# Moving the direct term of a state-space scan from VectorE to GpSimd and TensorE

## Chip, cores and metric

The kernel runs on one core of a Trainium2 chip. The metric is device time in microseconds for one launch; the runs shown are three executions of the same program. All arithmetic is in float32. Engine names in profile lines: PE is TensorE's matmul, PEld its weight load, DVE is VectorE, ACT is ScalarE, POOL is GpSimd, SP is SyncE with the DMA queue.

## What is computed

The reference runs two layers over 16 images of 128 channels and 56 x 56 pixels. The first is a vision block with windowed attention and an MLP. The change touches the second layer alone: a 3x3 convolution whose output, read as rows of 8 tokens of 16 values, goes through a small selective-scan (Mamba) block, then a group norm, a SiLU and a residual. Cut to what matters:

```python
def _mamba(seq, ...):
    xz = jnp.einsum('nld,ed->nle', seq, in_proj_w)
    xi, z = jnp.split(xz, 2, axis=-1)
    xc = ...                                   # causal conv over the tokens, then silu
    dt, Bm, Cm = ...                           # projections of xc; dt through softplus
    dA = jnp.exp(dt[..., None] * A)
    dBx = dt[..., None] * Bm[:, :, None, :] * xc[..., None]
    def step(h, inp):
        a, b, c = inp
        h = a * h + b
        return (h, jnp.sum(h * c[:, None, :], axis=-1))
    _, ys = jax.lax.scan(step, h0, ...)        # 8 tokens, 32 x 16 states
    ym = ys.transpose(1, 0, 2) + D * xc
    ym = ym * jax.nn.silu(z)
    return jnp.einsum('nld,ed->nle', ym, out_proj_w)
```

The state starts at zero, so at the first token the recurrence only injects. At the last token the state is not needed any more beyond the output. The kernel uses this: at tokens 0 and 7 the part of the output that comes from the token's own injection, `sum over s of C[s] * B[s] * dt * x`, is formed directly as `(sum of C*B) * (dt*x)`. This is the direct term, `ud` in the code.

## The kernel before

The second layer (`layer1`) works on 112 groups, 7 per image, each of 448 columns (a column is one sequence of 8 tokens). Each group takes 14 steps; step `k` of group `i` handles token `1 + k // 2` and half `k % 2` of the inner channels (`jp`). The 8 tokens lie in two halves `h` (tokens 0 to 3 and 4 to 7): tiles such as `dt`, `dtx`, `xc`, `zs`, `ym` are 128 x 2 x 448, and a partition holds one token of the half and one inner channel.

In every step, in this order:

- DVE: **advance** (L1001: decay times state, in PSUM; at token 7 L999 writes the product as the state), **complete** (L1006: adds the injected part; not at token 7), **inject** for four steps later (L991: the spread `dt*x` from PSUM times B).
- PE: **decay** for two steps later (L973, two matmuls on 32 rows each), **spread** for five steps later (L984, likewise).
- ACT: the exponential of the decay (L976, in place in PSUM).
- POOL, in odd steps: **weigh** (L1010: state times C, 128 x 1792).

Decay has two PSUM buffers and spread has one, so PE's spread waits for the injection before it, and the next injection waits for that spread.

Around these, `work(i, k)` returns lists for PE (with the ACT work that follows a matmul), DVE and POOL, which prepare the next groups and finish the last ones. The lists are issued in the step in which they are named, and `_chain` fixes program order on each engine, so the order by hand is the order on the engines. DVE's list stands after advance and before complete, except in step 0, where it stands after inject. With `prev`, `nxt` and `far` for the group before, the next one and the one after that, the parts are:

- steps 0, 1: `gather` of tokens 5, 6 and 7 of `prev` (L1019: sums over states into PSUM bank `pq[1]`); steps 1, 2: `rate` of `nxt` (L905); step 3: `gate` (L931), and `collect` of half 1 of `prev` (L1032); step 4: `gated` of half 1 (L1035, POOL), and `inner` for `zs` (L892, SiLU with a table load on ACT before and after, L146);
- steps 5, 6: `project_out` of `prev` (L1053); steps 5 to 9: nine convolution taps for the next image (L184); steps 6 and 8: `rate_sum`, four POOL products each (L922 to L925);
- step 7: `skip` of half 0 (L1025: a diagonal matmul adds `D * xc`, and starts the sum in `pq[1]`); steps 8, 9, 10: `gather` of tokens 1, 2, 3; steps 9, 10: `statistics` of the group norm (L1080) in groups that follow an odd or the last group of an image;
- step 10: `product` of `nxt` (L951, C times B); step 11: `sequences` (L884); step 12: `collect` of half 0 and `inner` for `xc` (table loads again); step 13: `direct` of `nxt` (L955: a matmul sums C times B over the states for tokens 0 and 7 into `pq[0]`), `skip` of half 1, `gather` of token 4, and `gated` of half 0.

`direct_mul` (L960), in step 0 on DVE, forms `ud` for both halves from `pq[0]`: bank times a column mask (`vec[:, 6 + h]`, 1 on the partitions of token 0 or of token 7) times `dtx`. `collect` adds `ud` to the gathered sum as it moves it from PSUM to `ym`; `gated` multiplies by `zs`, the SiLU of z.

In four of the seven groups of an image (groups 2 to 5, from the second image on) steps 4 and 12 also run a piece of the normalise-and-SiLU of the image before on ACT (L1121); POOL adds the residual in pieces (L1126). The last image has no convolution taps to run.

Of the kernel before, what the change touches and what calls it, by code (L numbers as in the profile page):

```python
# [10 lines left out]
F32 = mybir.dt.float32  # L11
U32 = mybir.dt.uint32
AF = mybir.ActivationFunctionType
ALU = mybir.AluOpType
# [3 lines left out]
P = 128  # L18
# [5 lines left out]
BLK = 448  # L24
NBLK = HW // BLK
# [113 lines left out]
def _load(nc, pool, ap, name):  # L139
    t = pool.tile(list(ap.shape), F32, tag=name, name=name)  # L140
    nc.sync.dma_start(t, ap)
    return t
# [653 lines left out]
def layer1(ctx: ExitStack, tc: tile.TileContext, x1, t, out, conv):  # L796
# [15 lines left out]
    nc = tc.nc  # L812
# [3 lines left out]
    cst = ctx.enter_context(tc.tile_pool(name="l1c", bufs=1))  # L816
    w1 = ctx.enter_context(tc.tile_pool(name="l1w1", bufs=1))
    w2 = ctx.enter_context(tc.tile_pool(name="l1w2", bufs=2))
# [14 lines left out]
    vec = conv.vec  # L833
    ident = _load(nc, cst, t["k_ident"], "ident1")
# [6 lines left out]
    for w, name in ((wx, "b_kx"), (wv, "b_dtw")):  # L841
        k = w1.tile(list(w.shape), F32, tag="fold", name=name)
# [3 lines left out]
    nc.vector.scalar_tensor_tensor(adec, adec, -1.0, mask, ALU.mult, ALU.mult)  # L846
    dd = cst.tile([P, P], F32, tag="dd", name="dd")
    nc.vector.tensor_scalar_mul(dd, ident, d_w)
    eps = cst.tile([P, 1], F32, tag="eps1", name="eps1")
    nc.vector.memset(eps, GN_EPS)  # L850
    neg = cst.tile([P, 1], F32, tag="neg", name="neg")
# [3 lines left out]
    pq = [ps_q.tile([P, 512], F32, tag=f"q{k}", name=f"pq{k}") for k in range(2)]  # L855
# [97 lines left out]
    def direct(p):  # L953

        nc.tensor.matmul(pq[0][:, 0:BLK], lhsT=cbm, rhs=p["cb"], start=True, stop=True)  # L955

    def direct_mul(p):
        ud = p["ud"] = w2.tile([P, 2, BLK], F32, tag="ud", name=f"ud_{p['n']}")
        for h in range(2):
            nc.vector.scalar_tensor_tensor(  # L960
                ud[:, h, :], pq[0][:, 0:BLK], vec[:, 6 + h : 7 + h], p["dtx"][:, h, :], ALU.mult, ALU.mult
            )

# [58 lines left out]
    def skip(p, h):  # L1024
        nc.tensor.matmul(  # L1025
            pq[1][:, 0:BLK], lhsT=dd, rhs=p["xc"][:, h, :], start=True, stop=False, skip_group_check=True
        )

    def collect(p, h):
        if h == 0:  # L1030
            p["ym"] = w1.tile([P, 2, BLK], F32, tag="ym", name=f"ym_{p['n']}")
        nc.vector.tensor_add(p["ym"][:, h, :], pq[1][:, 0:BLK], p["ud"][:, h, :])  # L1032

    def gated(p, h):
        nc.gpsimd.tensor_mul(p["ym"][:, h, :], p["ym"][:, h, :], p["zs"][:, h, :])  # L1035

    xrs = {}

# [70 lines left out]
    def residual(b, k):  # L1109
        pool, tag = (w2, "xr") if b == NB - 1 and k == 1 else (w1, "res")  # L1110
        res = norms[b, k] = pool.tile([P, half], F32, tag=tag, name=f"res_{b}_{k}")
        nc.sync.dma_start(res[0:64], x1[b][0:64, k * half : (k + 1) * half])
        if k == 0:
            nc.sync.dma_start(res[64:P], x1[b][64:P, 64 : half + 64])
        else:
            nc.sync.dma_start(res[64:P, 0 : half - 64], x1[b][64:P, half + 64 : HW])
            nc.sync.dma_start(res[64:P, half - 64 : half], x1[b][64:P, 0:64])
# [35 lines left out]
    def work(i, k):  # L1153


        def at(n):
            return groups[n] if 0 <= n < len(groups) else None

        p, nxt, far, prev = at(i), at(i + 1), at(i + 2), at(i - 1)
        pe, dve, pool = [], [], []  # L1160

        if prev:
            if k == 0:
                pe += [partial(gather, prev, 5), partial(gather, prev, 6)]
            if k == 1:
                pe.append(partial(gather, prev, 7))
            if k == 3:
                dve.append(partial(collect, prev, 1))
            if k == 4:
                pool.append(partial(gated, prev, 1))  # L1170
            if k in (5, 6):
                pe.append(partial(project_out, prev, k - 5))
            b = prev["b"]
            if prev["g"] % 2 and k in (9, 10):
                dve.append(partial(statistics, b, prev["g"] - 10 + k))
            if prev["g"] == NBLK - 1:
                if k == 9:
                    dve.append(partial(statistics, b, NBLK - 1))
                if k == 12 and b < NB - 1:
                    residual(b, 0)  # L1180
        two = at(i - 2)
        if two and two["g"] == NBLK - 1:
            b = two["b"]
            if k == 3:
                pool.append(partial(deviation, b))
        three = at(i - 3)
        if three and three["g"] == NBLK - 1:
            if k == 1:
                pe.insert(0, partial(group_var, three["b"], 0))
            if k == 2:  # L1190
                pool.append(partial(affine, three["b"]))
                if three["b"] == NB - 1:
                    pool.append(partial(finish, three["b"]))

        eighth = []
        for n in range(3, 7):
            past = at(i - n)
            if past and past["g"] == NBLK - 1 and past["b"] < NB - 1 and k in (4, 12):
                eighth.append(partial(normalise, past["b"], 2 * (n - 3) + k // 12))
        for n in range(4, 8):  # L1200
            past = at(i - n)
            if past and past["g"] == NBLK - 1 and past["b"] < NB - 1 and k == 2:
                pool.append(partial(store, past["b"], (n - 4) // 2, n % 2))
                if n == 5:
                    pool.append(partial(residual, past["b"], 1))

        if p:
            if i == len(groups) - 1 and k in (4, 6):
                residual(p["b"], k // 2 - 2)
            if k == 0:  # L1210
                dve.append(partial(direct_mul, p))
            if k == 7:
                pe.append(partial(skip, p, 0))
            if k in (8, 9, 10):
                pe.append(partial(gather, p, k - 7))
            if k == 12:
                dve.append(partial(collect, p, 0))
            if k == 13:
                if nxt:
                    pe.append(partial(direct, nxt))  # L1220
                pe += [partial(skip, p, 1), partial(gather, p, 4)]
                pool.append(partial(gated, p, 0))
            if k in (2, 6):
                bring(p, 0, {2: (4, 5), 6: (6,)}[k])
            if k in (1, 5, 9):
                bring(p, 1, {1: (3, 4), 5: (5, 6), 9: (7,)}[k])

        if nxt:
            if k in (1, 2):
                pe.append(partial(rate, nxt, k - 1))  # L1230
            if k in (2, 6):
                pe.append(partial(rate_exp, nxt, k // 4))
            if k in (5, 7):
                pe.append(partial(rate_log, nxt, k // 2 - 2))
            if k in (6, 8):
                pool.append(partial(rate_sum, nxt, k // 2 - 3))
            if k == 3:
                pe += [partial(gate, nxt, 0), partial(gate, nxt, 1)]
            if k == 4:
                eighth.insert(0, partial(inner, nxt, "zs", wz, w2, 0.0))  # L1240
            if k == 7:
                bring(nxt, 0, (0, 1))
            if k == 8:
                bring(nxt, 1, (1, 2))
            if k == 11:
                bring(nxt, 0, (2, 3))
            if k == 10:
                pool.append(partial(product, nxt))
            if k == 13 and not p:
                pe.append(partial(direct, nxt))  # L1250

        if p and k in (5, 6, 7, 8, 9) and p["b"] + 1 < NB:
            taps = {5: (0, 1), 6: (2, 3), 7: (4,), 8: (5, 6), 9: (7, 8)}[k]
            pe.append(partial(convolve, p["b"] + 1, p["g"], taps))
        if p and p["g"] == NBLK - 1 and k == 11 and p["b"] + 2 < NB:
            conv.load(p["b"] + 2)
        if two and two["g"] == NBLK - 1 and k == 2:
            pe.append(partial(group_mean, two["b"], 0))
        if far:
            if k == 11:  # L1260
                pe.append(partial(sequences, far))
            if k == 12:
                eighth.insert(0, partial(inner, far, "xc", wx, w3, c1_b))
        if eighth:
            pe = eighth + [partial(_act_set, tc, EXP_LN)] + pe
        return pe, dve, pool
# [10 lines left out]
    start = len(nc.cur_bb.bb.instructions)  # L1277
# [6 lines left out]
    for i in range(-2, len(groups) + 3):  # L1284
        for k in range(14):
            now = 0 <= i < len(groups)
            pe, dve, pool = work(i, k)
# [62 lines left out]
```

## Time and profile before

| | us |
|---|---|
| median of three runs | 8308.35 (8305.95 to 8310.39) |
| profiled execution, its own time | 8305.77 |
| its span, first to last instruction | 8304.0 |
| first and last `direct_mul` start (L960) | 3202.4, 8232.3 |
| mean of a POOL product 128 x 448 (L1035) | 1.145 |
| mean of a weighing 128 x 1792 (L1010) | 4.000 |
| mean of a residual addition 128 x 784 (L1126) | 1.854 |
| mean of a DVE product 128 x 896 (L1001) | 1.091 |
| mean of a statistics instruction (L1080) | 0.618 |
| mean of an ACT copy from PSUM 128 x 448 (L935) | 0.532 |

In lines of groups, after the shapes stand the count, the busy time in us and the mean of one in ns; after the second bar the idle time of the engine before these instructions and what ended it. In timelines a line gives start and duration in us, engine, line, operation, output from inputs, and in brackets the idle time before it. A float32 matmul shows as two records. Line numbers are those of the kernel before.

### The profile page before, as it was taken

To read this page: it belongs to the slowest core of one execution; us is meant where nothing else is said; L and a number is where in the kernel's file an instruction comes from. 1 tells how busy PE (TensorE), PEld (TensorE's weight loads), DVE (VectorE), ACT (ScalarE), POOL (GpSimd) and SP (SyncE) were. 2 spreads that over 40 slices of the span, in tenths; PEclk is the share of its full clock that TensorE was granted. 3 is DMA by queue.
4 is the path that set the end of the run, shared out by engine and by line. 5 is a ranking of instruction groups with operands and counts; after the bars stand their busy time and mean duration, and the time that the engine had idled before them with its cause. 6 is when DMAs were issued, how large, how long until landed. Compare 5 with 4: busy or idle time off the path is not lost.

```text
span 8304.0 us, 151471 instructions
## 1 busy us (share of the span) xinstructions
PE 7835.1 (94%) x52860; PEld 3329.9 (40%) x52860; DVE 7736.9 (93%) x10346; ACT 5642.6 (68%) x10579; POOL 7054.9 (85%) x5692
## 2 busy tenths in 40 slices
PE   5999999999999998999999999999999999999998
PEld 3444444444444453333333333333333333333332
DVE  7999999999999976999999999999999999999998
ACT  4777777777777755666666666666666666666665
POOL 7888788888888725899989999999999989999997
PEclk8999999999999999999999999999999999999998
DMA  3333333333333323333333334334333343334333
GB/s 65 87 86 87 85 89 87 87 87 87 87 87 87 81 79 82 87 93 102 99 92 99 96 91 105 91 97 106 83 104 100 88 105 103 86 99 108 85 93 88
DMA packets 764584, 757.87 MB, mean 91 GB/s; under 512 B 188720, under 2 KB 663984, under 8 KB 761904
## 3 DMA queue, kind: packets, MB, share of 16 engines
q1 hardware_dynamic: 763824, 748.18, 34.9%
q8 instruction: 423, 6.93, 0.4%
q14 instruction: 337, 2.76, 0.1%
HBM read 439.61 MB, written 102.76 MB: 65 GB/s over the span
## 4 chain that ended last, share of the span: by engine, by line
PE 34%; DVE 24%; POOL 24%; issue 9%; ACT 9%; DMA 1%; SPq 0%; POOLq 0%; ACTq 0%; DVEq 0%
PE a L973 7%; DVE h L991 6%; DVE a L1001 5%; POOL cst L1010 5%; PE x L984 5%; POOL xh L315 5%; PE pq L1019 5%; PE pq L892 4%; POOL e L431 4%; DVE h L1006 4%; DVE lepe L512 3%; POOL tap L313 3%; POOL dtx L925 2%; PE pq L931 2%; DVE sst L415 2%
## 5 line engine op out<-in xcount | busy, mean ns | idle before, releaser
L1010 POOL TENSOR_TENSOR cst<-h,cb 128x1792 f32<-128x1792 f32 x784 | 3130.6, 4000 | 348.9 <-DVE h L1006 291.1
L976 ACT ACTIVATE a<-a 128x896 f32<-128x896 f32 x1568 | 1415.7, 903 | 1080.2 <-PE x L984 588.0
L991 DVE TENSOR_TENSOR h<-x,bb 128x896 f32<-128x896 f32 x1568 | 1697.5, 1083 | 96.6 <-PE x L984 58.2
L512 DVE SCALAR_TENSOR_TENSOR lepe<-vpad,lep,lepe 128x448 f32<-128x448 f32 x2688 | 1718.0, 678 | 0.5
L984 PE MATMUL x<-dtx,amask 32*128 32x448 f32 x6272 | 1626.4, 595 | 49.0 <-DVE h L991 38.5
L973 PE MATMUL a<-dt,adec 32*128 32x448 f32 x6272 | 1620.2, 593 | 53.7 <-DVE h L1006 49.9
L1006 DVE TENSOR_TENSOR h<-a,h 128x896 f32<-128x896 f32 x1344 | 1463.1, 1089 | 38.1
L1001 DVE TENSOR_TENSOR a<-a,h 128x896 f32<-128x896 f32 x1344 | 1465.7, 1091 | 26.7 <-ACT a L976 25.8
L431 POOL TENSOR_SCALAR e<-e,sst,zero 128x256 f32<-128x256 f32 x1568 | 861.1, 559 | 466.6 <-DVE sst L427 417.4
L421 ACT ACTIVATE e<-ps,sst 128x256 f32<-128x256 f32 x1568 | 728.6, 469 | 522.5 <-DVE sst L415 470.5
L973 PEld LDWEIGHTS a<-dt,adec 32*128 32x128 f32 x6272 | 474.5, 185 | 1066.5 <-DVE h L1006 501.4
L315 POOL TENSOR_TENSOR xh<-xh,tap 128x448 f32<-128x448 f32 x749 | 859.6, 1148 | 43.7
L184 PE MATMUL pq<-pad,conv 128*128 128x448 f32 x1890 | 834.8, 559 | 0.0
L1019 PE MATMUL pq<-cst,sel 128*32 128x448 f32 x6272 | 734.5, 553 | 0.8 <-POOL cst L1010 0.8
L415 DVE TENSOR_REDUCE sst<-ps 128x2 f32<-128x512 f32 x784 | 540.3, 689 | 107.9 <-PE ps L409 83.0
L146 ACT ACT_TABLE_LOAD x484 | 621.0, 1283 | 9.3 <-PEq L1341 0.7
L453 PE MATMUL ptt<-ident,e 128*128 128x128 f32 x3136 | 538.6, 283 | 93.5 <-POOL e L431 76.8
L984 PEld LDWEIGHTS x<-dtx,amask 32*128 32x128 f32 x6272 | 476.7, 185 | 365.9 <-DVE h L991 344.3
L409 PE MATMUL ps<-sel,q 32*64 32x256 f32 x6272 | 537.3, 411 | 53.2 <-ACT e L421 46.9
L313 POOL TENSOR_SCALAR tap<-pad,pos,zero 128x448 f32<-128x448 f32 x749 | 546.5, 730 | 35.7
L453 PEld LDWEIGHTS ptt<-ident,e 128*128 128x128 f32 x3136 | 366.6, 141 | 417.5 <-POOL e L431 237.0
L459 ACT COPY att<-ptt 128x512 f32<-128x512 f32 x784 | 458.7, 585 | 72.0 <-PE ptt L453 64.1
(175 smaller groups left out, 12040.7 us busy)
## 6 DMA issues: line engine op xcount, KB each, us to landing
sel<-kv SPq DMA_DIRECT2D x3136, 64.0 KB
bb<-db SPq DMA_DIRECT2D x336, 448.0 KB
cb<-dc SPq DMA_DIRECT2D x336, 448.0 KB
pad<-x SPq DMA_DIRECT2D x32, 784.0 KB
x<-r SPq DMA_DIRECT2D x112, 224.0 KB
pad<-x SPq DMA_DIRECT2D x16, 1568.0 KB
db<-bs SPq DMA_DIRECT2D x112, 224.0 KB
dc<-cs SPq DMA_DIRECT2D x112, 224.0 KB
```

What stands on the lines that cost most here:

```text
L315: nc.gpsimd.tensor_add(im["xh"][i], im["xh"][i], held["tap"])
L431: nc.gpsimd.tensor_scalar(e, e, im["st", w][:, 2, p : p + 1], zero, ALU.mult, ALU.add)
L453: nc.tensor.transpose(ptt[:, P * (2 * p + h) : P * (2 * p + h + 1)], e[:, h * P : (h + 1) * P], ident)
L512: nc.vector.scalar_tensor_tensor(out, src, lep[:, k : k + 1], acc, ALU.mult, ALU.add)
L973: nc.tensor.matmul(a[:, k, :], lhsT=adec[rows, l4, :], rhs=p["dt"][rows, h, :], start=True, stop=True)
L976: nc.scalar.activation(p["a", l, jp], p["a", l, jp], AF.Exp)
L984: nc.tensor.matmul(x[:, k, :], lhsT=mask[rows, l4, :], rhs=p["dtx"][rows, h, :], start=True, stop=True)
L991: nc.vector.tensor_mul(p["h", l][:, own(jp), :], px["x"], weight)
L1001: nc.vector.tensor_mul(a, a, before)
L1006: nc.vector.tensor_add(h, p["a", l, jp], h)
L1010: nc.gpsimd.tensor_mul(c, p["h", l], p["gate", 1, l].unsqueeze(1).to_broadcast([P, 4, BLK]))
L1019: nc.tensor.matmul(py[32 * j : 32 * j + 32], lhsT=sel[:, l4, :], rhs=p["c", l][:, j, :], start=False, stop=(l % 4 == 3), skip_group_check= ...
```

## The change

Three things are changed in the second layer.

1. `direct` copies its bank to an SBUF tile `cbs` on ACT right after the matmul. `direct_mul` becomes one POOL product of 128 x 2 x 448, `dtx` times `cbs`, without the mask, still in step 0.
2. The mask becomes a diagonal matrix per half, `ends[:, h, :]`, made once. `skip` issues a second matmul with it, which adds the masked `ud` to `pq[1]`. `collect` then multiplies the bank with `zs` instead of adding `ud`, and `gated` and its two calls go.
3. `statistics` moves from steps 9 and 10 to step 13 and to step 0 of the group after.

```diff
+    ends = cst.tile([P, 2, P], F32, tag="ends", name="ends")
+    for h in range(2):
+        nc.vector.tensor_scalar_mul(ends[:, h, :], ident, vec[:, 6 + h : 7 + h])
...
         nc.tensor.matmul(pq[0][:, 0:BLK], lhsT=cbm, rhs=p["cb"], start=True, stop=True)
+        p["cbs"] = w1.tile([P, BLK], F32, tag="cbs", name=f"cbs_{p['n']}")
+        nc.scalar.copy(p["cbs"], pq[0][:, 0:BLK])

     def direct_mul(p):
-        ud = p["ud"] = w2.tile([P, 2, BLK], F32, tag="ud", name=f"ud_{p['n']}")
-        for h in range(2):
-            nc.vector.scalar_tensor_tensor(
-                ud[:, h, :], pq[0][:, 0:BLK], vec[:, 6 + h : 7 + h], p["dtx"][:, h, :], ALU.mult, ALU.mult
-            )
+        p["ud"] = w1.tile([P, 2, BLK], F32, tag="ud", name=f"ud_{p['n']}")
+        nc.gpsimd.tensor_mul(p["ud"], p["dtx"], p["cbs"].unsqueeze(1).to_broadcast([P, 2, BLK]))
...
             pq[1][:, 0:BLK], lhsT=dd, rhs=p["xc"][:, h, :], start=True, stop=False, skip_group_check=True
         )
+        nc.tensor.matmul(
+            pq[1][:, 0:BLK], lhsT=ends[:, h, :], rhs=p["ud"][:, h, :], start=False, stop=False, skip_group_check=True
+        )
...
-        nc.vector.tensor_add(p["ym"][:, h, :], pq[1][:, 0:BLK], p["ud"][:, h, :])
-
-    def gated(p, h):
-        nc.gpsimd.tensor_mul(p["ym"][:, h, :], p["ym"][:, h, :], p["zs"][:, h, :])
+        nc.vector.tensor_mul(p["ym"][:, h, :], pq[1][:, 0:BLK], p["zs"][:, h, :])
...
-            if k == 4:
-                pool.append(partial(gated, prev, 1))
...
-            if prev["g"] % 2 and k in (9, 10):
-                dve.append(partial(statistics, b, prev["g"] - 10 + k))
             if prev["g"] == NBLK - 1:
-                if k == 9:
-                    dve.append(partial(statistics, b, NBLK - 1))
...
         two = at(i - 2)
+        if prev and prev["g"] % 2 and k == 13:
+            dve.append(partial(statistics, prev["b"], prev["g"] - 1))
+        if two and (two["g"] % 2 or two["g"] == NBLK - 1) and k == 0:
+            dve.append(partial(statistics, two["b"], two["g"]))
...
             if k == 0:
-                dve.append(partial(direct_mul, p))
+                pool.append(partial(direct_mul, p))
...
-                pool.append(partial(gated, p, 0))
```

## The prediction

> **What bounds the kernel now.** I read the engine totals first, then the groups of instructions on the lines the change touches, then the timelines of single groups in the second layer, and last the granted clock in windows of a few us.
>
> ```profile
> PE 7835.1 (94%) x52860; PEld 3329.9 (40%) x52860; DVE 7736.9 (93%) x10346; ACT 5642.6 (68%) x10579; POOL 7054.9 (85%) x5692
> ...
> L991 DVE TENSOR_TENSOR h<-x,bb 128x896 f32<-128x896 f32 x1568 | 1697.5, 1083 | 96.6 <-PE x L984 58.2 <-POOL cst L1010 18.4 <-DMA bb<-db 3.9
> ```
>
> PE and DVE are both near full. Shares do not say which one a step waits for, so the steps must be read. The first product of a group starts at 3202.4 us and that of the 112th at 8232.3: 45.31 us a group, all of it in the second layer, which alone is changed.
>
> ```profile
> L960 DVE SCALAR_TENSOR_TENSOR ud<-pq,vec,dtx 128x448 f32<-128x448 f32 x224 | 141.9, 675 | 0.6 <-PE pq L955 0.6
> L1035 POOL TENSOR_TENSOR ym<-ym,zs 128x448 f32<-128x448 f32 x224 | 256.5, 1145 | 0.7 <-DVE ym L1032 0.7
> ```
>
> These two rows are what leaves DVE and POOL. Consecutive DVE instructions overlap a little, so the time that the two products of a group take up is read from starts: 5014.19 to 5015.38, 1.19 us.
>
> ```profile
> 5007.84 1.09 DVE L991 TENSOR_TENSOR h<-x,bb 128x896 f32<-128x896 f32 x1
> ...
> 5013.20 1.08 DVE L991 TENSOR_TENSOR h<-x,bb 128x896 f32<-128x896 f32 x1
> 5014.19 1.27 DVE L960 SCALAR_TENSOR_TENSOR ud<-pq,vec,dtx 128x448 f32<-128x448 f32 x2
> 5015.38 1.09 DVE L1001 TENSOR_TENSOR a<-a,h 128x896 f32<-128x896 f32 x1
> ```
>
> ```profile
> 5010.00 1.28 ACT L146 ACT_TABLE_LOAD   x1
> 5011.29 1.16 ACT L893 ACTIVATE xc<-pq,vec 128x448 f32<-128x448 f32 x2
> 5012.34 0.71 ACT L1121 ACTIVATE xr<-xr,gst 128x392 f32<-128x392 f32 x1
> 5013.07 1.28 ACT L146 ACT_TABLE_LOAD   x1
> 5014.36 0.90 ACT L976 ACTIVATE a<-a 128x896 f32<-128x896 f32 x1
> ```
>
> This is one group that also normalises a piece of the image before (L1121). After the two products DVE goes on with the advance of step 1 at 5015.38; the exponential that this advance reads ends on ACT at 5014.36 + 0.90 = 5015.26. The products hide a chain (table load, two SiLU, normalise, table load, exponential) that ends 0.12 us before them. These groups take 45.26 us, and a second cycle closes them: POOL's weighing of token 5 starts at 5003.81, takes 4.00, and the injection at 5007.84 starts as it ends.
>
> Groups without a normalise piece take 44.67 to 44.83 us. There PE is the neighbour:
>
> ```profile
> 5193.00 0.91 PE L1025 MATMUL pq<-xc,dd 128*128 128x448 f32 x2
> 5193.84 0.96 PE L1019 MATMUL pq<-cst,sel 128*32 128x448 f32 x8
> ...
> 5194.74 0.65 PE L984 MATMUL x<-dtx,amask 32*128 32x448 f32 x2
> ```
>
> ```profile
> 5184.34 1.09 DVE L991 TENSOR_TENSOR h<-x,bb 128x896 f32<-128x896 f32 x1 [0.24 <-PE x L984]
> 5185.62 1.09 DVE L999 TENSOR_TENSOR h<-a,h 128x896 f32<-128x896 f32 x1 [0.19 <-ACT a L976]
> ```
>
> A full matmul of 448 columns takes PE 0.85 us from start to start (5193.00 to 5193.84). At steps 11 and 12 DVE already waits 0.43 us for work that PE reaches late after the convolution taps of steps 5 to 9.
>
> **What the change costs, by part.** Per group:
> - Removed from DVE: the two products, 1.19 us. The two collections stay one DVE instruction each, of the same shape with one PSUM operand, 0.615 us either way.
> - POOL: two gatings go (2 x 1.145 = 2.29), one product of 896 elements comes. No row has that shape; the neighbours are 784 elements at 1.85 (L1126) and 1792 at 4.00 (L1010). Those are its bounds; on the line between them it is 2.1, near the lower row, and I take that. So POOL gets 0.2 us lighter (1.7 heavier at the upper bound, less than the 2.9 us that POOL idles between 4705 and 4717). The output chain loses its POOL hop: the project-out of steps 5 and 6 waits for DVE alone. The new product stands on POOL ahead of the weighing of token 1, where a gating stood (5016.77).
> - ACT: one copy of 448 columns from PSUM, 0.53 (as L935), after the exponential of step 13. It reads the matmul that ended at 5013.46 and is over before the exponential of step 0, which starts at 5016.26 after 1.00 us of waiting. Cover: that wait. Without it, 0.53.
> - PE: two more full matmuls, 0.85 each, at the end of step 7 (before a tap) and in step 13 (before the gather of token 4). Behind them in PE's order stand the decay and spread of the next step, which DVE waits for. Their new wait for POOL's product should cost nothing: the product can run from 5016.77 and end near 5019, the skip of step 7 stands at 5039.69; the cover is those 20 us.
> - Statistics (0.53 each between starts) move from between advance and complete of steps 9 and 10, where they cost 0.40 (5000.53 to 5001.06, less the 0.13 that the pair advance-complete then saves), to steps 13 and 0.
> - Two constant tiles at the start: 2 x 0.29 us (as L848). Nothing.
>
> Now the path, group by group.
> (a) Normalising groups (60 of 112). The advance of step 1 may start at 5015.26 plus the 0.05 that such a hand-over takes, instead of 5015.38. Gain 0.07, about nothing; the statistics now stand inside this wait and are free. I take 0.
> (b) Plain groups, steps 13 to 1, from the group at 5190. Without the products the injection of step 1 would go from 5197.05 to 5195.86. ACT lets the advance start at 5194.18, so injection 5196.30. PE's spread of step 0, at 5194.74 before, comes 0.85 later, 5195.59; with 1.02 + 0.05 until DVE sees it, 5196.66. Gain 5197.05 - 5196.66 = 0.38, with or without statistics in steps 13 and 0 (0.33 to 0.79 us, inside the slack). 1.14 for the three plain groups of an image.
> (c) Plain groups, steps 5 to 12. PE's work in steps 5 to 9: 3.62, 3.62, 2.67, 3.56, 3.56 = 17.03 us (0.97 for decay and spread side by side; 0.95 project-out, 0.85 per tap or skip, 0.89 per gather), against DVE's 5 x 3.13 = 15.65 (5015.38 to 5018.51 is one step). With the second skip matmul PE has 17.88. In the group without statistics the 0.43 wait grows by 0.85. In the two with statistics DVE had its own work there, which goes: 0.80 (two statistics), and 0.73 (one, with the aggregate of 0.345, L1082, less overlap); the loss is 0.85 - (0.80 - 0.43) = 0.48, and 0.55. Sum 1.88 for three groups.
> (d) Net for three plain groups: +0.74 us. Over 14 images and the seven plain groups of the first: 14 x 0.74 + 1.7 = +12. Lag carried into the first normalising group: between 0 and the 0.43 of (c), I take 0.2: +3. The last image has no taps, so (c) falls away: -1. Sum +14 us.
> (e) The clock.
>
> ```profile
> 4732.63:4736.04 3.41, 2.52 (x13) 0.97 (x12) 2.72 (x5) 2.85 (x4) 3.41 (x3) 1.00 0.00 0
> 4736.04:4739.46 3.42, 3.42 (x8) 1.32 (x11) 3.12 (x3) 1.22 (x3) 3.42 (x2) 0.50 0.00 0
> ```
>
> Columns: window, PE, PEld, DVE, ACT, POOL busy, granted clock, DMA share, GB/s. For 3.4 us the clock is halved, just after a window in which PE was busy only 2.52 of 3.41; in it PE idled 0.89 us at step 12, waiting for the injection that POOL releases. The group that holds it takes 46.55 instead of 45.26. From 4514 to 6554 seven groups carry such an excess, 12.5 us together, so some 29 us over 15 images; six of the seven are at or next to such a step 12. With the extra matmul PE arrives there 0.85 later and the 0.89 gap closes. That gives 0 to -25 us; I take -18.
>
> [...]
>
> **Sum.** The profiled execution took 8305.77 (span 8304.0 and 1.8 around it), 2.6 under the median 8308.35. 8305.8 + 14 - 18 = 8302 for it, 8304 as a median.
>
> **Rivals.**
> - DVE bounds every group and its 1.19 us are won whole: 112 x 1.19 = 133, 8175. For it: DVE busy 97% in the second layer and hardly any wait before it. Against: ACT's chain ends 0.12 us before the products do. 5%.
> - The lag of (c) is absorbed (PE catches up in the light steps 10 and 11) while (b) and the clock pay fully: -18 - 25, 8265. For it: those steps hold 1.86 and 1.67 us of PE work against 3.13. Against: 0.43 us of waiting there today. 20%.
> - Slower: PE becomes the bound through the 1.7 us it gains per group. Place: injection and advance at steps 9 to 12 and 1. Price: (c) whole, without (b), 1.88 x 16 = 30, and 6 carried over, clock as before: 8344; with (b) and no change of the clock 8322. It decides from the point where the clock wins less than (d) costs. 32%.
> - My forecast, the two nearly cancel: 43%.
>
> A measurement of this kernel tells 0.2% (17 us) from no change. The forecast and the milder half of the slower rival lie within it; slower by more takes 0.32 (a part of the forecast's own spread included), faster 0.27, same 0.41. The range: low end by the second rival, 8268; high end short of the slower one's worst, 8338. The forecast's own: 8290 to 8320.
>
> **What would show it.** Right: in normalising groups DVE waits some 1.1 us for ACT before the advance of step 1, group time still about 45.3; in plain groups waits for PE's x around steps 9 to 12 of more than 1 us, group time about 45.0; fewer windows with clock 0.5; POOL's new product near 2.1 us. Wrong: group times near 44 (first rival), or group times above 45.6 with PE never idle (slower), or a product on POOL far above 2.1 that delays the weighing.

## The result, and the profile after

| | us |
|---|---|
| changed kernel, median of 12 runs | 8301.76 (8290.64 to 8310.63) |
| kernel before, median of 12 runs in the same comparison | 8306.0 (8304.29 to 8310.39) |
| ratio, with 95% interval | 0.9994 [0.9986, 1.0003] |
| profiled execution of the changed kernel, and its span | 8302.31, 8300.2 |
| mean granted TensorE clock of the two profiled executions, before and after | 0.983, 0.986 |

No change that can be told from none. The forecast was 8304. That the time stands still although VectorE (DVE) lost 100 us of work is what has to be explained. Even the 4 us between the two profiled executions lie outside what was changed: the second layer, from step 4 of its first group to step 4 of its last, takes 5030.14 us before and 5031.29 after, and the changed kernel enters it 4.0 us earlier, out of a first layer that the change does not touch (the stretch behind is 1.0 us shorter).

The engine totals, the shares of the chain of waits, and the groups of instructions of the changed kernel (line numbers are three higher than before in this part of the code):

```profile
PE 7836.6 (94%) x53308; PEld 3359.1 (40%) x53308; DVE 7635.4 (92%) x10124; ACT 5693.8 (69%) x10691; POOL 7034.5 (85%) x5580
PE 52%; DVE 18%; POOL 15%; ACT 8%; issue 7%; DMA 0%; SPq 0%; POOLq 0%; DVEq 0%; ACTq 0%
```

```profile
L965 POOL TENSOR_TENSOR ud<-dtx,cbs 128x896 f32<-128x896 f32 x112 | 236.3, 2110 | 14.9 <-ACT cbs L961 11.9 <-PE pq L1031 3.0
L1031 PE MATMUL pq<-ud,ends 128*128 128x448 f32 x448 | 210.9, 553 | 0.0
L994 DVE TENSOR_TENSOR h<-x,bb 128x896 f32<-128x896 f32 x1568 | 1697.4, 1083 | 133.3 <-PE x L987 104.3 <-DMA bb<-db 15.7 <-POOL cst L1013 0.5
L1004 DVE TENSOR_TENSOR a<-a,h 128x896 f32<-128x896 f32 x1344 | 1465.2, 1090 | 72.2 <-ACT a L979 68.5
```

Two rows of the kernel before, to set beside these:

```profile
PE 34%; DVE 24%; POOL 24%; issue 9%; ACT 9%; DMA 1%; SPq 0%; POOLq 0%; ACTq 0%; DVEq 0%
L1001 DVE TENSOR_TENSOR a<-a,h 128x896 f32<-128x896 f32 x1344 | 1465.7, 1091 | 26.7 <-ACT a L976 25.8
```

DVE is busy 101.5 us less and idles about as much more: before the injection (L994) it waits 104.3 us for PE's spread, 58.2 before, and before the advance (L1004) 68.5 us for ACT's exponential, 25.8 before. Two places take in 89 of the 101.5 us. The wait for POOL in the injection fell from 18.4 us to 0.5, and one for the load of B rose from 3.9 to 15.7. PE's share of the chain that ended last went from 34% to 52%. The product on POOL takes 2.11 us.

A normalising group, first DVE, then ACT (same kernel, timeline; in brackets the idle time before):

```profile
4962.47 1.08 DVE L994 TENSOR_TENSOR h<-x,bb 128x896 f32<-128x896 f32 x1
4964.50 1.10 DVE L1004 TENSOR_TENSOR a<-a,h 128x896 f32<-128x896 f32 x1 [0.95 <-ACT a L979]
```

```profile
4961.56 0.70 ACT L1124 ACTIVATE xr<-xr,gst 128x392 f32<-128x392 f32 x1
4962.28 1.28 ACT L146 ACT_TABLE_LOAD   x1
4963.57 0.90 ACT L979 ACTIVATE a<-a 128x896 f32<-128x896 f32 x1
4964.38 0.54 ACT L961 COPY cbs<-pq 128x448 f32<-128x448 f32 x1
```

Where the two products stood, DVE now waits 0.95 us: the advance starts 0.03 us after the exponential ends (4963.57 + 0.90 = 4964.47), 0.12 us after it before. The new copy (L961) stands behind that exponential and holds nothing up. These groups take 45.21 us, 45.26 before. (Group times here and below run from the injection that DVE issues in step 4 to the same injection of the next group.)

A group without a normalise piece, DVE and PE:

```profile
4860.68 1.09 DVE L994 TENSOR_TENSOR h<-x,bb 128x896 f32<-128x896 f32 x1 [0.39 <-PE x L987]
4864.17 1.09 DVE L994 TENSOR_TENSOR h<-x,bb 128x896 f32<-128x896 f32 x1 [0.27 <-PE x L987]
4865.45 1.09 DVE L1002 TENSOR_TENSOR h<-a,h 128x896 f32<-128x896 f32 x1 [0.19 <-ACT a L979]
```

```profile
4872.60 0.92 PE L1028 MATMUL pq<-xc,dd 128*128 128x448 f32 x2
4873.35 0.92 PE L1031 MATMUL pq<-ud,ends 128*128 128x448 f32 x2
4874.20 0.96 PE L1022 MATMUL pq<-cst,sel 128*32 128x448 f32 x8
```

At steps 10 to 12 DVE waits 0.85 us in three pieces (the last one for an exponential), against 0.43 before. The new matmul takes 0.85 us from start to start (4873.35 to 4874.20). Plain groups without a halving of the clock take 44.92 to 45.15 us, 44.64 to 44.85 before. So all groups now stand near 45.1, each kind at its own limit. An image of seven such undisturbed groups takes 315.3 us before and 316.1 after.

What the clock did: the full-speed time lost to a granted clock of 0.5 in windows of 2 us from 3400 to 7960 us, divided by the 1.71 that one halving loses, makes 20 halvings before and 7 after. What they cost can be read from the groups. In images 2 to 15 the groups together take 30 us more than undisturbed ones before, and 13 after; about 1 us of each is a wait for the load of B (`bb`, see below). That leaves 29 us for 20 halvings and 12 for 7, so 1.4 and 1.7 us each. These counts are of one execution per kernel. The mean granted clock of the 12 runs of the changed kernel is 0.984 to 0.987, that of 19 runs of the kernel before 0.981 to 0.984.

One stall has grown. In the group that follows the four normalising ones (group 6 of an image) DVE waits for the load of B in every image from the second on, 0.4 to 1.8 us and 3.7 in the last; before there were three such waits, 0.4, 0.9 and 2.6 us. It costs little here: that group takes 45.15 us in twelve of images 2 to 15, and 45.8 and 45.9 in two. SyncE's queue and DVE in one of these two:

```profile
4747.50 0.52 SPq L1132 DMA_DIRECT2D out<-xr  x1
4748.07 0.59 SPq L1133 DMA_DIRECT2D out<-xr  x1
4748.71 2.66 SPq L1134 DMA_DIRECT2D out<-xr  x1
4751.47 2.33 SPq L941 DMA_DIRECT2D db<-bs  x1
...
4757.08 2.98 SPq L947 DMA_DIRECT2D bb<-db  x2
```

```profile
4764.48 1.09 DVE L994 TENSOR_TENSOR h<-x,bb 128x896 f32<-128x896 f32 x1 [1.77 <-DMA bb<-db]
```

The image's output (128 x 3136 values, 1.6 MB) leaves in one burst when its last residual piece is added, and the stores and loads of the next group's B (`db`, `bb`) are issued right behind it.

### The profile page after: what moved, and what is told of

Read it like the earlier page. It is cut to its first block, busy times and chain, and to the rows that moved or that the text cites. A ratio compares the mean times of both kernels' runs of the same rounds, so it can differ in the third digit from the quotient of the medians.

```text
span 8300.2 us, 152052 instructions
## 1 busy us (share of the span) xinstructions
PE 7836.6 (94%) x53308; PEld 3359.1 (40%) x53308; DVE 7635.4 (92%) x10124; ACT 5693.8 (69%) x10691; POOL 7034.5 (85%) x5580
## 4 chain that ended last, share of the span: by engine, by line
PE 52%; DVE 18%; POOL 15%; ACT 8%; issue 7%; DMA 0%; SPq 0%; POOLq 0%; DVEq 0%; ACTq 0%
PE a L976 12%; PE pq L184 9%; PE pq L1022 6%; POOL xh L315 5%; POOL e L431 4%; PE x L987 4%; PE pq L896 4%; DVE h L994 3%; POOL tap L313 3%; DVE lepe L512 3%; PE pq L1056 3%; PE pq L935 2%; PE pq L1028 2%; DVE a L1004 2%; PE pq L1031 2%
## 5 line engine op out<-in xcount | busy, mean ns | idle before, releaser
L994 DVE TENSOR_TENSOR h<-x,bb 128x896 f32<-128x896 f32 x1568 | 1697.4, 1083 | 133.3 <-PE x L987 104.3
L987 PE MATMUL x<-dtx,amask 32*128 32x448 f32 x6272 | 1622.6, 593 | 40.7 <-DVE h L994 31.2
L976 PE MATMUL a<-dt,adec 32*128 32x448 f32 x6272 | 1618.4, 592 | 38.7 <-DVE h L1009 36.7
L1004 DVE TENSOR_TENSOR a<-a,h 128x896 f32<-128x896 f32 x1344 | 1465.2, 1090 | 72.2 <-ACT a L979 68.5
L409 PE MATMUL ps<-sel,q 32*64 32x256 f32 x6272 | 534.9, 409 | 51.5 <-ACT e L421 45.5
```

Source lines behind the costliest of these rows:

```text
L976: nc.tensor.matmul(a[:, k, :], lhsT=adec[rows, l4, :], rhs=p["dt"][rows, h, :], start=True, stop=True)
L987: nc.tensor.matmul(x[:, k, :], lhsT=mask[rows, l4, :], rhs=p["dtx"][rows, h, :], start=True, stop=True)
L994: nc.vector.tensor_mul(p["h", l][:, own(jp), :], px["x"], weight)
L1004: nc.vector.tensor_mul(a, a, before)
```

## The experiments

Medians; every ratio is to the kernel before, which was run beside it. "Halvings" are counted as above.

**The wall behind DVE.** First the products alone: before, without them.

```diff
     def direct_mul(p):
-        ud = ...
-        for h in range(2):
-            nc.vector.scalar_tensor_tensor(...)
+        p["ud"] = nought
```

> The kernel before without the two products on DVE; the collection adds a constant zero tile, so the output lacks the direct term. This is what leaves DVE, without what comes to PE, ACT and POOL. My theory: normalising groups stay at about 45.2 (mean 45.26 before), since ACT's exponential ends 0.12 us before the products did; plain groups gain some 0.7 us each: 8306 - 49 x 0.7 - 4 = about 8268 (8250 to 8285). Rival 'DVE sets the time': 112 x 1.19 = 133 us less, 8173. Rival 'PE sets the time': 8306.

8264.14 us (8249.02 to 8277.9), ratio 0.9943 [0.9927, 0.996]. DVE's 1.19 us in 112 groups are 133 us; with nothing put in their place 41 come out (8305.42 - 8264.14). Without a halving, normalising groups stay at 45.1 to 45.2 and plain ones stand at 43.9 to 44.1. The clock is halved 32 times instead of 20 in the profiled execution, which was the slowest of the four (8277.9 us, clock 0.979; the others 0.982 to 0.984). The advance now waits for ACT's exponential, 113.0 us instead of 25.8:

```profile
L999 DVE TENSOR_TENSOR a<-a,h 128x896 f32<-128x896 f32 x1344 | 1465.6, 1091 | 113.0 <-ACT a L974 113.0
```

So the products did hold the plain groups, and in the normalising ones ACT's chain lies close behind.

Next PE's addition alone: before, with a matmul of zero weights after each `skip`.

```diff
+        nc.tensor.matmul(
+            pq[1][:, 0:BLK], lhsT=noughts, rhs=p["xc"][:, h, :], start=False, stop=False, skip_group_check=True
+        )
```

> The kernel before with a second matmul of zero weights after each skip matmul, in the places where the change puts its own; nothing is left out. This is what comes to PE alone. My theory: plain groups go from 44.7 to about 45.4, 49 x 0.7 = 34 us, normalising ones change by at most 0.1, and the halvings of the clock after step 12 go, -15 to -25: about 8320 (8305 to 8340), with fewer windows at clock 0.5 than the kernel before has. Rival 'PE sets the time everywhere': 190 us more, 8496. Rival 'PE is hidden': 8306.

8318.17 us (8312.33 to 8321.73), ratio 1.0015 [1.0005, 1.0024]. Its DVE timeline in a plain group:

```profile
4872.44 1.09 DVE L993 TENSOR_TENSOR h<-x,bb 128x896 f32<-128x896 f32 x1 [0.39 <-PE x L986]
4875.94 1.09 DVE L993 TENSOR_TENSOR h<-x,bb 128x896 f32<-128x896 f32 x1 [0.27 <-PE x L986]
4877.22 1.09 DVE L1001 TENSOR_TENSOR h<-a,h 128x896 f32<-128x896 f32 x1 [0.19 <-ACT a L978]
```

These are the same three waits, to the hundredth, that the changed kernel has: the two matmuls alone are enough to make them. Nearly all groups stand at 45.34 to 45.5 and the clock is halved once. The cost is 13 us (8318.17 - 8305.42), after what the clock gives back.

The changed kernel without its two new matmuls:

```diff
-        nc.tensor.matmul(
-            pq[1][:, 0:BLK], lhsT=ends[:, h, :], rhs=p["ud"][:, h, :], start=False, stop=False, skip_group_check=True
-        )
```

> The changed kernel without the two matmuls with the diagonal mask, so the output lacks the direct term; everything else stays. My theory (two walls): in normalising groups ACT's chain sets the time, so they stay at 45.2 us; in plain groups PE's extra 1.7 us set it, so they fall from 44.9-45.15 to about 44.2, some 49 x 0.8 = 40 us, of which the clock takes back about 10 because PE idles at step 12 again: about 8268 (8250 to 8285). Rival 'DVE sets the time': DVE's work is unchanged, so 8302. Rival 'PE sets the time everywhere': 112 x 1.7 = 190 us less, 8112.

8288.65 us (8282.48 to 8297.32), ratio 0.9983 [0.9973, 0.9993]: above the range that was expected. Undisturbed plain groups fall to 43.9 to 44.4 and normalising ones to 45.10, both close to what was expected. What the expectation had too small is the clock: 28 halvings instead of the changed kernel's 7, which cost some 39 us instead of 12 by the groups of images 2 to 15, where 10 us more were assumed. Its row of the injection and two DVE waits from one normalising group:

```profile
L994 DVE TENSOR_TENSOR h<-x,bb 128x896 f32<-128x896 f32 x1568 | 1695.0, 1081 | 127.5 <-PE x L987 74.6 <-POOL cst L1013 35.1 <-DMA bb<-db 8.6
```

```profile
4943.26 1.09 DVE L994 TENSOR_TENSOR h<-x,bb 128x896 f32<-128x896 f32 x1 [0.56 <-POOL cst L1013]
4950.64 1.10 DVE L1004 TENSOR_TENSOR a<-a,h 128x896 f32<-128x896 f32 x1 [0.95 <-ACT a L979]
```

The wait for POOL's weighing before the injection of step 12, which PE's longer work had covered (0.5 us in the whole changed kernel), is back at 35.1 us. Why this kernel is 24 us above the one without the products, with as little on DVE and PE, was not separated; they differ in the copy on ACT, in POOL's load and in where the statistics stand.

**The normalising groups.** The changed kernel with no normalise pieces in the loop, and that together with the edit above:

```diff
-            if past and past["g"] == NBLK - 1 and past["b"] < NB - 1 and k in (4, 12):
-                eighth.append(partial(normalise, past["b"], 2 * (n - 3) + k // 12))
```

> The changed kernel without the normalise pieces on ACT (L1124 there) and the two or so table loads they do not need otherwise stay; the group norm and its SiLU are left out for all images but the last. My theory: with ACT's chain 0.7 us shorter in steps 4 and 12 the normalising groups meet the other wall, PE, and fall from 45.21 only to about 45.05: 56 x 0.16 = 9 us less, 8293 (8280 to 8303). Rival 'ACT's chain is the one wall': they fall to the 44.3 that DVE's own work allows, 56 x 0.9 = 50 us less, 8252.

> The changed kernel without the normalise pieces and without the matmuls with the diagonal mask: both walls away; the direct term, and the group norm with its SiLU for all images but the last, are left out. My theory: now DVE's saving shows, all groups fall to 43.9 to 44.3, about 105 x 0.95 = 100 us, of which the clock takes back 10 to 25 as PE idles more: about 8220 (8195 to 8245). If the walls were independent, the parts would add: -13 (measured without the mask matmuls) and -9: 8280.

Without the pieces alone: 8283.15 us (8272.6 to 8288.61), ratio 0.9972 [0.9961, 0.9984]; all groups fall to 44.92 to 45.15 and no further. Without pieces and matmuls: 8199.77 us (8194.14 to 8207.88), ratio 0.9875 [0.9858, 0.9891]; groups take 43.9 to 44.4 where the clock is not halved, but group 6 takes 45.2 to 45.8, with waits for B of 1.2 to 1.8 us. The rows of the kernel without the pieces, then those of the one without both:

```profile
L1004 DVE TENSOR_TENSOR a<-a,h 128x896 f32<-128x896 f32 x1344 | 1463.9, 1089 | 26.7 <-ACT a L979 26.4
L994 DVE TENSOR_TENSOR h<-x,bb 128x896 f32<-128x896 f32 x1568 | 1697.8, 1083 | 152.6 <-PE x L987 115.6 <-DMA bb<-db 13.2 <-POOL cst L1013 2.0
```

```profile
L1004 DVE TENSOR_TENSOR a<-a,h 128x896 f32<-128x896 f32 x1344 | 1463.8, 1089 | 22.9 <-ACT a L979 22.9
L994 DVE TENSOR_TENSOR h<-x,bb 128x896 f32<-128x896 f32 x1568 | 1695.7, 1081 | 92.0 <-PE x L987 55.0 <-DMA bb<-db 22.1 <-POOL cst L1013 4.0
```

The matmuls alone are worth 13 us (8301.76 - 8288.65), the pieces alone 19, both together 102. Of the 70 us by which both exceed the sum, some 31 stand in undisturbed groups: against the changed kernel's 316.1 us an undisturbed image takes 2.9 us less without the matmuls, 1.0 less without the pieces and 6.1 less without both, so 2.2 more than the sum, in 14 images. Most of the rest is the clock: 28 halvings without the matmuls alone, 5 without the pieces, 7 with both gone, 7 in the changed kernel. The 31 us are what two limits in parallel look like: in a normalising group ACT's chain sets 45.1 and PE's work 44.9 to 45.0, and taking one away shows the other. Without the pieces the wait for ACT drops from 68.5 us to 26.4, but that for PE rises from 104.3 to 115.6. Without the matmuls PE's drops to 74.6, but ACT's stays at 70.2 and POOL's comes back. Only with both gone do both drop, to 22.9 and 55.0.

**The statistics.** The changed kernel with them back in steps 9 and 10:

```diff
+            if prev["g"] % 2 and k in (9, 10):
+                dve.append(partial(statistics, b, prev["g"] - 10 + k))
...
-        if prev and prev["g"] % 2 and k == 13:
-            dve.append(partial(statistics, prev["b"], prev["g"] - 1))
```

> The changed kernel with the statistics back in steps 9 and 10; nothing is left out. My theory: DVE waits in both places (for PE around steps 9 to 12, for ACT or PE at step 1), so the place does not matter: 8302 (8290 to 8315). Rival 'the place of the statistics is what made the change break even': their 0.4 us come back in each of the 112 groups, 8347.

8304.99 us (8299.71 to 8308.6), ratio 0.9998 [0.9988, 1.0007]. The move costs and brings nothing that can be measured. That fits the waits seen above, for PE beside steps 9 and 10 and for ACT before step 1, in which these instructions find room.

**The clock.** Before, with one matmul of zero weights at step 12 of groups 3 and 5, into a free bank, where PE idled 0.89 us:

```diff
                 decay(*decays)
+            if now and k == 12 and groups[i]["g"] in (3, 5):
+                nc.tensor.matmul(pq[0][:, 0:BLK], lhsT=noughts, rhs=groups[i]["xc"][:, 0, :], start=True, stop=True)
             if further:
```

> The kernel before with one more matmul of zero weights, 0.85 us, in step 12 of groups 3 and 5 of an image, between decay and spread, where PE idled 0.89 us; its result is overwritten. Nothing is left out. My theory: the halvings of the clock come from that idle time, so they fall from 20 windows to under 8 in the steady part and the time by 15 to 25 us though PE does more: 8285 (8278 to 8296). Rival 'the clock follows something else': 8306 or, where the matmul delays the spread, up to 8320.

8287.12 us (8277.72 to 8293.18), ratio 0.9975 [0.9966, 0.9985], 3 halvings instead of 20. PE at step 12 of such a group:

```profile
4727.20 1.02 PE L975 MATMUL a<-dt,adec 32*128 32x448 f32 x4
4728.15 1.02 PE L1307 MATMUL pq<-xc,noughts 128*128 128x448 f32 x2
4729.10 1.02 PE L986 MATMUL x<-dtx,amask 32*128 32x448 f32 x4
```

The filler (L1307) closes the gap between decay and spread; nothing is computed with it, and the kernel is 20 us faster (8307.52 - 8287.12). This shows step (e) by itself: it is the idle gap, not the work, that costs. In the changed kernel this gap is 0.25 us. What PE waits for the injection before its spreads (L984 in the kernel before) sums to 38.5 us before, 31.2 in the changed kernel and 30.1 in the kernel before with zero-weight matmuls after each `skip`.

Not every such gap halves the clock; where it falls decides. The onsets of the halvings lie on one grid of 3.413 us. Between 3400 and 7960 us the kernel before has 28 gaps of 0.88 to 0.91 us ahead of the spread of step 12: the 16 that begin 1.2 to 2.3 us behind a grid point are followed by a halving at the next one, the 12 that begin less than 0.2 or more than 2.8 us behind one are not. The changed kernel has only one gap of over 0.7 us an image left, 1.3 to 1.6 us in group 0; its 7 halvings follow 7 of these 14, the ones that begin 1.2 to 1.94 us behind a grid point, where 2 of 14 did before. How many do is the luck of the grid.

**One matmul instead of two.** If PE is the limit of the plain groups, the mask and `D` can go elsewhere: ACT applies the mask in the copy and scales `xc` by `D` in place, POOL adds the two, and one matmul with the identity is left.

```diff
-        nc.scalar.copy(p["cbs"], pq[0][:, 0:BLK])
+        for h in range(2):
+            nc.scalar.activation(p["cbs"][:, h, :], pq[0][:, 0:BLK], AF.Identity, scale=vec[:, 6 + h : 7 + h])
...
+        nc.gpsimd.tensor_add(p["ud"], p["ud"], p["xc"])
...
-            pq[1][:, 0:BLK], lhsT=dd, rhs=p["xc"][:, h, :], start=True, stop=False, skip_group_check=True
-        )
-        nc.tensor.matmul(
-            pq[1][:, 0:BLK], lhsT=ends[:, h, :], rhs=p["ud"][:, h, :], start=False, stop=False, skip_group_check=True
+            pq[1][:, 0:BLK], lhsT=ident, rhs=p["ud"][:, h, :], start=True, stop=False, skip_group_check=True
```

> The changed kernel with one skip matmul per half instead of two: ACT applies the mask while it copies (two copies), scales xc by D in place in step 10, POOL adds it to the direct term, and PE sums the result with the identity. Nothing is left out. PE is back at its work before, POOL has 2.1 us more per group out of 2.9 us idle, ACT 1.4 more. My theory: as without the mask matmuls, normalising groups 45.1, plain ones 44.1 to 44.3, the clock halved as often: 8288 (8275 to 8305). Rival 'POOL becomes the bound': its weighings come 2 us later and the normalising groups go above 46, over 8340.

8332.01 us (8322.88 to 8339.42), ratio 1.0031 [1.0018, 1.0043]: a miss of 44 us. Normalising groups take 45.12 and plain ones 43.9 to 44.4 where nothing disturbs them, as expected. But the first normalising group of an image takes 46.3 us or more, group 6 takes 46.4 to 51.5, with waits of 2.4 to 4.3 us for the load of B in most images (12 waits of 41.4 us in all, the longest 6.8), and the clock is halved 38 times. The same with the rate's logarithm and its POOL products for half 0 two steps earlier:

```diff
-            if k in (5, 7):
-                pe.append(partial(rate_log, nxt, k // 2 - 2))
-            if k in (6, 8):
-                pool.append(partial(rate_sum, nxt, k // 2 - 3))
+            if k in (3, 7):
+                pe.append(partial(rate_log, nxt, k // 4))
+            if k in (4, 8):
+                pool.append(partial(rate_sum, nxt, k // 4 - 1))
```

> The kernel with one skip matmul, and the first half of the rate sum earlier: its ACT part in step 3 (before the table switch of step 4) instead of 5, its POOL part in step 4 instead of 6. Nothing is left out. My theory: the cycle that closes the normalising groups runs from ACT's table loads through POOL's eight rate products and two weighings to the injection of step 12; starting POOL earlier opens it, so the 0.56 us wait for POOL before step 12 goes and with it PE's idle time and most halvings of the clock: normalising groups about 44.7, 8265 (8235 to 8285). Rival 'ACT's chain alone sets 45.1': no change against the kernel with one skip matmul.

8245.92 us (8234.91 to 8250.36), ratio 0.9927 [0.991, 0.9943], 15 halvings. Normalising groups fall to 44.46, all four of an image, and group 6 still takes 46.1 to 50.8. Two injections of one group 6:

```profile
4743.44 1.09 DVE L993 TENSOR_TENSOR h<-x,bb 128x896 f32<-128x896 f32 x1 [3.09 <-DMA bb<-db]
...
4750.90 1.09 DVE L993 TENSOR_TENSOR h<-x,bb 128x896 f32<-128x896 f32 x1 [1.11 <-PE x L986]
```

Here B comes 3.09 us late, and PE, stalled with DVE, late again behind it. Then the output is stored in four pieces, each as its residual piece is ready, in this kernel and in the changed one:

```diff
-        if k == q == 1:
-            xr = xrs[b]
-            nc.sync.dma_start(outv[b, 0], xr[0:64])
-            nc.sync.dma_start(outv[b, 1, :, 64:HW], xr[64:P, 0 : HW - 64])
+        lo = k * half + q * half // 2
+        hi = lo + half // 2
+        xr, last = xrs[b], k == q == 1
+        nc.sync.dma_start(outv[b, 0, :, lo:hi], xr[0:64, lo:hi])
+        if last:
             nc.sync.dma_start(outv[b, 1, :, 0:64], xr[64:P, HW - 64 : HW])
+        end = HW - 64 if last else hi
+        nc.sync.dma_start(outv[b, 1, :, lo + 64 : end + 64], xr[64:P, lo:end])
```

> The kernel with one skip matmul and the early rate, and the finished image now leaves in four pieces, each as soon as POOL has added its residual, instead of all 1.6 MB after the last. Nothing is left out. My theory: in the group after the four normalising ones the injection waits 2.4 to 3.2 us for B from DRAM because the output transfer, issued when POOL's last piece ends, fills the DMA engines just then, and PE's idle time there halves the clock; with pieces that wait goes: about 15 x 3.5 us less, 8195 (8180 to 8215). Rival 'the queue waits for POOL anyway, not for the bytes': 8246 stays.

> The changed kernel with the image leaving in four pieces. Nothing is left out. My theory: the waits of 0.4 to 1.8 us for B are there already but mostly stand inside the PE wall, so only the 0.15 to 0.9 us per image by which that group exceeds 45.2 go: 15 x 0.3 = 5 us less, 8297 (8288 to 8304). Rival 'they are on the path': 15 x 0.9 = 14 us less, 8288.

With one matmul: **8192.09 us** (8191.32 to 8196.38), ratio 0.9865 [0.9849, 0.9881], faster than both kernels of this case. SyncE's queue at the end of an image, to set beside that of the changed kernel:

```profile
4715.99 0.51 SPq L1129 DMA_DIRECT2D out<-xr  x1
4716.55 0.59 SPq L1131 DMA_DIRECT2D out<-xr  x1
4717.19 0.59 SPq L1133 DMA_DIRECT2D out<-xr  x1
4717.88 0.64 SPq L935 DMA_DIRECT2D db<-bs  x1
```

A quarter of the output leaves here, and the store of B behind it is issued in 0.64 us instead of 2.33. Group 6 takes 44.39 us, the waits for B between 3400 and 7960 us sum to 0.33 us, and the clock is halved 4 times. So the late rate (86 us from 8332.01 to 8245.92) and the burst of stores (another 54) were what made the one-matmul kernel slow.

The changed kernel with the same stores: 8297.76 us (8293.14 to 8301.42), ratio 0.999 [0.998, 0.9999]; 4 us under 8301.76, near what was expected, though from different comparisons whose intervals overlap. No wait for B is left in its trace. Images 2 to 15 take 3.1 us less there than in the trace of the changed kernel: one halving fewer, and 1.4 us in the two groups 6 that had exceeded 45.15.

## Why the prediction was right, step by step

- (a) Normalising groups, no gain: right. DVE waits 0.95 us for ACT where about 1.1 was forecast, the group takes 45.21 us where 45.3 was. The kernel without the two matmuls, in which these groups keep 45.10, shows that ACT's chain is a limit. The kernel without the pieces, in which they keep 44.9 to 45.0, shows that PE's work is a second one close by, which the prediction did not say.
- (b) and (c) Plain groups: right in sum, not in the parts. Groups 6, 0 and 1 take 45.14, 45.10 and 45.01 us, before 44.77, 44.68 and 44.83: 0.97 us more in sum, 0.74 forecast. For (b), from the injection of step 0 to that of step 1 it is 3.87 us (4872.34 to 4876.21), 4.32 before (5192.73 to 5197.05): a gain of 0.45, 0.38 forecast. For (c), the wait at steps 10 to 12 of group 1, which has no statistics, grew by 0.42 (0.43 to 0.85), where 0.85 was forecast and "more than 1 us" named as the sign; the two groups with statistics lost more than forecast, about 0.4 each net of (b) where 0.10 and 0.17 were.
- (d) The net, forecast +14: right for its main term, with two small ones wrong. The undisturbed image is 0.8 us longer, 11 us in 14 images, and the first image takes 1.4 more, where +12 was forecast for both. The 3 us of lag carried into the first normalising group are not seen; that group takes 45.21 like the others. The last image, taken at -1, is 5.9 us longer in the profiled execution (277.8 against 271.9 for six groups), where DVE waits for PE's spread; why was not followed up.
- (e) The clock, taken at -18: right, 17 by the groups (29 to 12), and shown by the filler alone (-20, 3 halvings) and by the zero-weight matmuls in the change's own places (one halving). In the kernel before the halvings follow stretches of 3.41 us in which PE was busy 2.1 to 2.5 us, and closing the gap at step 12 with the filler takes them from 20 to 3. That the net met -18 is in part the luck of the grid: the 16 onsets behind the closed gap are gone, and 5 more came behind the gap in group 0.
- The total: in the pair of profiled executions these make 1.4 + 11 + 5.9 - 17, about +1 us in the second layer, where -4 was forecast. That the medians differ by 4.2 us, almost exactly as forecast, is in part luck: the runs of the changed kernel spread over 20 us. What the record supports is the two terms and that they nearly cancel.
- Prices: POOL's product 2.11 us (2.1 taken), the copy on ACT 0.54 (0.53), the matmul 0.85 (0.85), the statistics nothing (nothing).
- Not foreseen: the load of B behind the burst of output. The prediction followed each queue that the change moves work past, but this stretch of SyncE's queue the change does not touch. In the changed kernel it costs 1.4 us in images 2 to 15; with one matmul the burst costs some 54. Why B comes later against its injection than it did before was not isolated.
- The rivals. "DVE bounds every group" (8175) falls by the kernel without the products, which wins 41 of 133 us though nothing is put in their place. "The lag is absorbed" (8265) falls by the three waits in the plain groups. The slower rival's mechanism is real, as the zero-weight matmuls show (+13), but the clock paid for it. Two terms of opposite sign that nearly cancel were the forecast; the small total says nothing of their size, and each had to be shown by itself.

## What to carry to other kernels

Before moving work off a busy engine, look at what ends just before that work does: here an exponential on ACT ended 0.12 us before the products, a spread on PE was next, and only taking both away (102 us, against 13 and 19 alone) showed what the move could be worth. When a stage has several limits close together, here 45.1 and 45.0 us, a relief pays in full only together with the next ones: against the kernel before, the change with one skip matmul, an earlier rate and spread-out stores gave 115 us together (8307.52 - 8192.09) where the first of them alone lost 27 (8332.01 - 8305.36). A burst of stores at the end of an image is worth splitting where loads stand behind it: in four pieces it gave 54 us with one matmul, and in the changed kernel 4, which its interval does not tell from none.

## What the hardware showed

- The clock falls to 0.5 for 3.41 us (in 2 of 18 cases before, twice that) after a stretch in which PE idled, 0.9 us or more of it in the kernel before. The onsets of these 18, over 4300 us, lie on one grid of 3.413 us. Where a gap falls decides whether it costs anything: of 28 PE gaps of 0.88 to 0.91 us in the kernel before, the 16 that begin 1.2 to 2.3 us behind a grid point are followed by a halving and the 12 others are not. Why these positions, the record does not show. With a matmul of zero weights in such a gap the halvings fall from 20 to 3 and the kernel before gains 20 us.
- Taking work from DVE or PE can bring halvings: 20 before and 32 without the products; 7 after, 28 without the two new matmuls, 38 with one matmul. It need not: 4 with one matmul and the stores in pieces. In images 2 to 15 the halvings cost some 39 us without the two new matmuls and 12 in the changed kernel, so part of what less work should win was lost there.
- A 1.6 MB store just ahead makes the store of B slow to issue, 2.0 to 2.4 us at the end of images 2 to 15 of the changed kernel and 2.0 to 2.2 before, against 0.64 with the store in four pieces. DVE then waits 0.4 to 1.8 us for the load of B in images 2 to 15 of the changed kernel and 3.0 us on average with one matmul and the early rate (13 waits, 38.7 us, beside one of 18.4 in its trace); with the pieces these waits are gone between 3400 and 7960 us but for one of 0.33 us, and one of 18.3 stays outside that stretch.
